# First-image statistics from the framed blocks, and three small reorderings in a convolution-attention and expert kernel

## The chip, the cores and the metric

The kernel runs on one core of one Trainium2 chip. The metric is device time in microseconds (us) of one execution, as a median over runs. Inputs come from HBM and the result goes back to HBM; everything is float32.

## The reference

The input `x` has 4 images of 256 channels and 64 x 64 pixels. Cut to what matters:

```python
# layer 0: group norm, then instance norm, then 3x3 neighbourhood attention
x = x + conv_attn(_gn(x), Wq, bq, Wk, bk, Wv, bv, Wo, bo)
#   xn = (x - mean over h,w) * rsqrt(var over h,w + eps)     per image and channel
#   q = (xn @ Wq + bq) / sqrt(256); k, v = padded xn @ Wk + bk, @ Wv + bv
#   softmax over the 9 neighbours, ctx @ Wo + bo
# layer 1, on 16384 tokens of 256 numbers
t = t + windowed_gated_mean(_ln_t(t), Wp, bp, Wg)             # last 64 tokens
t = t + moe(_ln_t(t), router_w, w1, b1, w2, b2)               # 8 experts, top 2
```

For this change the per-channel mean and variance of a whole image matter: nothing of an image's attention can be computed before all its 4096 pixels per channel have been seen. The kernel folds the two norms of layer 0 and the weights together (`qk` = Wq Wk', `vo` = Wv Wo, `outb` = bo + Wo' bv), and takes the token norm's mean out of the projection by subtracting the weights' own mean over channels (`wpr`).

## The kernel before, in words

An image is cut into 8 blocks of 8 rows (512 pixels), 32 blocks in all. Channels lie on the 128 partitions in two halves (`NC` = 2). A block's pixels come in three layouts, each with its own load on SyncE's queue (SP): `xs` (L151 to L161), 2 x 512 plain pixels per partition, 512 KB, used only for the statistics; `x` (L129 to L139), the block framed by its neighbours, 2 x 10 x 66 per partition, 660 KB, used by the attention; and `xp` (L141 to L146), patches with pixels on partitions, 1 MB.

`channel_stats` (L163) takes `bn_stats` of each channel half of one block on VectorE (DVE); `image_norm` (L420) aggregates the 8 blocks of an image (L423), averages over groups with two small matmuls by `gavg` (L427, L434), takes an inverse square root in some ten tiny DVE steps, and scales `qk` and `ub` by it. Its last part is the "shift products" (L455 to L466): 4 matmuls by `qk` and 8 by `ub`, each over one column (`back` = -mean times the inverse deviation), into the PSUM tile `pqb`; DVE adds them to `qb` and `qbk` (L467 to L470). `edges` (L476) writes the image's mean into the frame of the `x` tile on GpSimd (POOL) and into the patches by DMA.

Then each round of the main loop (L1163) interleaves, step by step, the attention of block g (`attend`), the ranking and dispatch of block g-2 (`ranks`), the windowed layer of block g-1 (`tail`), the queries of block g+1 (`produce`), and a share of the expert slots (`experts`). The expert part scatter-adds its rows to the output with indirect DMAs from POOL (L1094).

What sets the order. Engines run their own instruction streams in order. The tile framework's scheduler makes these streams from the program order and a running priority number; a smaller number goes first among what it believes ready (`tc.cur_priority`). `tc.keep_in_program_order` and `add_manual_dep(... NoSync ...)` only fix an order. DMAs of the SP and ScalarE (ACT) queues share 8 completion semaphores in turn, so the ninth of them isn't issued until the first has landed, and so on: at the start SP's loads and ACT's loads of weights wait for one another in that way.

The start of the kernel is a stage of its own. SP issues the 8 `xs` loads of image 0 (L176 to L178, into the idle buffers of the pools `xs`, `x1`, `wx` and `q`), then 4 `x` loads (L179), a blank block, and two `xp` loads. ACT issues the weights (L190 to L203). TensorE (PE) forms the folded weights (`product`, L387 to L413), which ACT and, for `outb` (L406) and `wpr` (L415), DVE move out of PSUM. DVE has the statistics, the masks (L241 to L261) and these in one stream.

Of the kernel before, what the change touches and what calls it, by code (L numbers as in the profile page):

```python
# [47 lines left out]
AF = mybir.ActivationFunctionType  # L48
# [14 lines left out]
def hybrid_block_kernel(ctx: ExitStack, tc: tile.TileContext, ins: dict, out: bass.AP):  # L63
    nc = tc.nc
    x = ins["x"]
    B, C, FW, _ = x.shape
    W = FW - 2
# [4 lines left out]
    NBI = HW // TB  # L72
# [6 lines left out]
    XBUFS = 4  # L79
    TH, TW = TB // W, 4  # L80
# [31 lines left out]
    xsp = ctx.enter_context(tc.tile_pool(name="xsp", bufs=2))  # L112
    xp = ctx.enter_context(tc.tile_pool(name="xp", bufs=XBUFS))
    xtp = ctx.enter_context(tc.tile_pool(name="xtp", bufs=2))
    xpp = ctx.enter_context(tc.tile_pool(name="xpp", bufs=2))
    w1p = ctx.enter_context(tc.tile_pool(name="w1p", bufs=1))
    w2p = ctx.enter_context(tc.tile_pool(name="w2p", bufs=2))
# [9 lines left out]
    xt, xpat = {}, {}  # L127

    def load_x(g):  # L129

        if g >= NB:
            return
        b, i = divmod(g, NBI)
        t = xp.tile([P, NC, KH, FW], FP, tag="x", name=f"x_{g}")
        nc.sync.dma_start(
            t.rearrange("p c h w -> p c (h w)"),
            x[b, :, i * TH : i * TH + KH, :].rearrange("(c p) h w -> p c (h w)", p=P),
        )
        xt[g] = t  # L139
# [6 lines left out]
        xpat[g] = t  # L146

    xs_of, stats = {}, {}
    idle = (xsp, "xs"), (xtp, "x1"), (w2p, "wx"), (w2p, "q")

    def load_xs(g):  # L151
        if g >= NB:
            return
        b, i = divmod(g, NBI)

        pool, tag = idle[g // 2] if g < NBI else idle[0]
        t = pool.tile([P, NC, TB], FP, tag=tag, name=f"xs_{g}")
        nc.sync.dma_start(
            t, ins["xs"][b, :, i * TB : (i + 1) * TB].rearrange("(c p) n -> p c n", p=P)
        )  # L160
        xs_of[g] = t  # L161

    def channel_stats(g):  # L163

        if g >= NB:
            return
        b, i = divmod(g, NBI)
        t = xs_of.pop(g)
        if i == 0:
            stats[b] = w2p.tile([P, NC, NBI, 6], FP, tag="stats", name=f"stats_{b}")  # L170
        for c in range(NC):
            inst = nc.vector.bn_stats(stats[b][:, c, i, :], t[:, c, :])
            if b:
                tc.keep_in_program_order(inst)

    for g in range(NBI):  # L176
        load_xs(g)
        channel_stats(g)  # L178
    for g in range(XBUFS):  # L179
        load_x(g)  # L180

    def load_const(name, shape, src):
        t = const.tile(shape, FP, tag=name, name=name)
        nc.scalar.dma_start(t, src)
        return t
# [10 lines left out]
    outb = load_const("outb", [P, NC], ins["bo"])  # L196
    A = ins["WpT"].shape[1]

    wpr = const.tile([P, NC, A + E], FP, tag="wpr", name="wpr")
# [65 lines left out]
    for n in range(2):  # L265
        t = const.tile([P, NG, HALF], FP, tag=f"pe_{n}", name=f"pe_{n}")
# [92 lines left out]
    def rsqrt_v(out_, var, eps, n, name):  # L359

        def four(tag, dtype=FP):
            return w4p.tile([P, 4], dtype, tag=tag, name=f"{tag}_{name}")[:, :n]

        ve, guess, t = four("nve"), four("guess", I32), four("nt")
        nc.vector.tensor_scalar_add(ve, var, eps)
        nc.vector.tensor_single_scalar(guess, ve.bitcast(I32), 1, op=ALU.arith_shift_right)
        nc.vector.tensor_scalar(guess, guess, -1.0, float(0x5F3759DF), ALU.mult, ALU.add)
        y = guess.bitcast(FP)
        for last in (False, False, True):
            nc.vector.tensor_mul(t, y, y)  # L370
            nc.vector.scalar_tensor_tensor(t, t, -0.5, ve, ALU.mult, ALU.mult)
            new = out_ if last else y
            nc.vector.scalar_tensor_tensor(new, t, 1.5, y, ALU.add, ALU.mult)
# [13 lines left out]
    def product(dst, pairs, n, name):  # L387
        ps = ps_a.tile([P, n], FP, tag="a", name=f"pw_{name}")
        for k, (lhsT, rhs) in enumerate(pairs):
            nc.tensor.matmul(ps, lhsT, rhs, start=(k == 0), stop=(k == NC - 1))  # L390
        return ps

    for c in range(NC):
        cols = slice(c * P, (c + 1) * P)
        both = range(NC)
        ps = product(qk, [(wqT[:, o, cols], wkT[:, o, :]) for o in both], C, f"qk{c}")
        nc.scalar.mul(qk[:, c, :], ps, SCALE)
        ps = product(qb, [(wkT[:, o, cols], bq[:, o : o + 1]) for o in both], 1, f"qb{c}")
        nc.scalar.mul(qb[:, c : c + 1], ps, SCALE)
        ps = product(vo, [(wvT[:, o, cols], wo[:, o, :]) for o in both], C, f"vo{c}")  # L400
        nc.scalar.copy(vo[:, c, :], ps)
        ps = product(ucol, [(wqT[:, o, cols], bk[:, o : o + 1]) for o in both], 1, f"u{c}")
        nc.scalar.mul(ucol[:, c : c + 1], ps, SCALE)
        nc.gpsimd.tensor_copy(ub[:, c, :], ucol[:, c : c + 1].to_broadcast([P, 32]))
        ps = product(outb, [(wo[:, o, cols], bv[:, o : o + 1]) for o in both], 1, f"outb{c}")
        nc.vector.tensor_add(outb[:, c : c + 1], outb[:, c : c + 1], ps)  # L406
    ps = product(qbk, [(bqb[:, o, :], bk[:, o : o + 1]) for o in range(NC)], 1, "qbk")
    nc.scalar.mul(qbk, ps, SCALE)

# [2 lines left out]
    nc.gpsimd.memset(mean_c, 1.0 / C)  # L412
    ps = product(wpr, [(mean_c, wpr[:, ci, :]) for ci in range(NC)], A + E, "wpr")  # L413
    for ci in range(NC):
        nc.vector.tensor_sub(wpr[:, ci, :], wpr[:, ci, :], ps)  # L415


    norm, mean_row, ask = {}, {}, {}
# [1 line left out]
    def image_norm(b):  # L420
        mv = w2p.tile([P, NC, 2], FP, tag="imv", name=f"imv_{b}")
        for c in range(NC):
            nc.vector.bn_aggr(mv[:, c, :], stats[b][:, c].rearrange("p i s -> p (i s)"))  # L423
        mean = w2p.tile([P, NC], FP, tag="imean", name=f"imean_{b}")
        nc.vector.tensor_copy(mean, mv[:, :, 0])
        gm = ps_a.tile([P, NC], FP, tag="a", name=f"gm_{b}")
        nc.tensor.matmul(gm, gavg, mean, start=True, stop=True)  # L427

        spread = w2p.tile([P, NC], FP, tag="ispread", name=f"ispread_{b}")
        nc.vector.tensor_sub(spread, mean, gm)  # L430
        nc.vector.tensor_mul(spread, spread, spread)
        nc.vector.tensor_add(spread, spread, mv[:, :, 1])
        gv = ps_a.tile([P, NC], FP, tag="a", name=f"gv_{b}")
        nc.tensor.matmul(gv, gavg, spread, start=True, stop=True)  # L434


        vc = w2p.tile([P, NC], FP, tag="ivc", name=f"ivc_{b}")
        nc.vector.scalar_tensor_tensor(vc, gv, EPS, mv[:, :, 1], ALU.mult, ALU.add)
        rc = w2p.tile([P, NC], FP, tag="irc", name=f"irc_{b}")
        rsqrt_v(rc, vc, EPS * EPS, NC, f"c{b}")  # L440
        back = w2p.tile([P, NC], FP, tag="iback", name=f"iback_{b}")
        nc.vector.scalar_tensor_tensor(back, mean, -1.0, rc, ALU.mult, ALU.mult)
        norm[b] = (mean, rc, back)
        row = mean_row[b] = hbm.tile([1, C], FP, tag=f"mean_row_{b}", name=f"mean_row_{b}")
        nc.sync.dma_start(row.rearrange("o (c p) -> p (o c)", p=P), mean)


        qks = w2p.tile([P, NC, C], FP, tag="qks", name=f"qks_{b}")
        ubs = w2p.tile([P, NC, 32], FP, tag="ubs", name=f"ubs_{b}")
        for c in range(NC):  # L450
            nc.scalar.mul(qks[:, c, :], qk[:, c, :], rc[:, c : c + 1])
            nc.gpsimd.tensor_scalar_mul(ubs[:, c, :], ub[:, c, :], rc[:, c : c + 1])
        qbb = w2p.tile([P, NC], FP, tag="qbb", name=f"qbb_{b}")
        ps = ps_a.tile([P, NC + 1], FP, tag="a", name=f"pqb_{b}")
        for co in range(NC):  # L455
            for ci in range(NC):
                nc.tensor.matmul(
                    ps[:, co : co + 1], qk[:, ci, co * P : (co + 1) * P], back[:, ci : ci + 1],
                    start=(ci == 0), stop=(ci == NC - 1),
                )  # L460
        for n in range(NG):
            for ci in range(NC):
                nc.tensor.matmul(
                    ps[32 * n : 32 * (n + 1), NC:], ub[:, ci, :], back[:, ci : ci + 1],
                    start=(ci == 0), stop=(ci == NC - 1),
                )  # L466
        nc.vector.tensor_add(qbb, qb, ps[:, 0:NC])  # L467
        nc.vector.tensor_mul(qbb, qbb, rc)
        kb = w2p.tile([P, 1], FP, tag="kb", name=f"kb_{b}")
        nc.vector.tensor_add(kb, qbk, ps[:, NC:])  # L470
        ask[b] = qks, qbb, ubs, kb
# [663 lines left out]
    for g in range(2):  # L1135
        load_xp(g)
    image_norm(0)
    edges(0)
    edges(1)
# [21 lines left out]
    for g in range(*stats_at[0]):  # L1161
        load_xs(g)
# [79 lines left out]
```

## Time and profile before

| | us |
|---|---|
| median of 19 runs (lowest to highest) | 1299.82 (1295.74 to 1303.95) |
| the profiled execution, its own time | 1305.36 |
| its span, first to last instruction | 1303.7 |
| PE busy, share of the span | 1140.2, 87% |
| DVE busy | 926.8, 71% |
| ACT busy | 824.4, 63% |
| POOL busy | 703.4, 54% |
| mean granted TensorE clock | 0.953 |

The profiled execution is 5.5 us above the median and 1.4 us above the highest of the runs. A line of the timeline has the start, the duration, the engine, the source line, the operation, output <- inputs with shapes, and in square brackets the idle time of that engine just before, with what ended it. SPq is SyncE's queue of DMA issues; PEld is the weight load of a matmul. A float32 matmul has two records.

### The profile page before, as it was taken

What the parts mean: (1) busy time and instruction counts of PE and PEld (TensorE: products, weight loads), DVE (VectorE), ACT (ScalarE), POOL (GpSimd) and SP (SyncE); (2) the same over time, 40 slices, a digit from 0 to 9 for tenths busy, and PEclk for the clock granted to TensorE, in tenths of its full rate; (3) what the DMA queues carried; (4) which work ended last, traced back from release to release, by engine and by line L of the source; (5) the groups of instructions that cost most, each with busy time, mean ns of one, the idle gap of its engine ahead of it and who ended that gap; (6) DMA issues with size and microseconds to landing.
All of it is one profiled execution on the core that took longest, in us unless ns stands there. A gap on an engine that the chain in (4) does not pass through costs nothing. (4 is left out here: it accounts for less than half of the span.)

```text
span 1303.7 us, 28100 instructions
## 1 busy us (share of the span) xinstructions
PE 1140.2 (87%) x8620; PEld 813.9 (62%) x8620; DVE 926.8 (71%) x4650; ACT 824.4 (63%) x1633; POOL 703.4 (54%) x615
## 2 busy tenths in 40 slices
PE   4977879999999999999999999999999999767660
PEld 4544556666767767676766676667676666656550
DVE  4488878978888888788878688878876798422220
ACT  1454557768777867787877678787867775423320
POOL 2013233666665657565656566666675667654443
PEclk9988879999999999999999899999999999878995
DMA  9774556777776777767777576667756556755543
GB/s 325 225 249 152 169 163 163 189 192 179 171 191 134 185 209 174 179 177 185 172 156 177 131 181 163 168 171 164 179 111 141 116 125 124 178 110 84 83 63 36
DMA packets 138723, 209.99 MB, mean 161 GB/s; under 512 B 15712, under 2 KB 108752, under 8 KB 134352
## 3 DMA queue, kind: packets, MB, share of 16 engines
q1 hardware_dynamic: 84912, 135.81, 34.2%
q0 software_dynamic: 51168, 71.07, 30.0%
q8 instruction: 71, 1.16, 0.4%
q10 hardware_dynamic: 2496, 1.32, 0.4%
q14 instruction: 76, 0.62, 0.2%
HBM read 117.56 MB, written 90.59 MB: 160 GB/s over the span
## 5 line engine op out<-in xcount | busy, mean ns | idle before, releaser
L1094 POOL DMA_INDIRECT out<-sx x270 | 427.9, 1585 | 380.2 <-DVE sx L1081 108.6
L892 POOL DMA_INDIRECT rows_in<-tok,rows x256 | 254.9, 996 | 139.8 <-issue 74.4
L1076 PE MATMUL psy<-w,h 128*128 x1080 | 292.5, 394 | 30.5 <-DVE sx L1080 29.1
L1076 PEld LDWEIGHTS psy<-w,h 128*128 128x128 f32 x1080 | 196.6, 193 | 126.5 <-DVE sx L1080 60.5
L1057 PE MATMUL psh<-xc,w1s 128*128 128x256 f32 x1080 | 271.5, 394 | 2.8 <-ACT h L1063 2.5
L1080 DVE TENSOR_TENSOR sx<-psy,b2b 128x256 f32<-128x256 f32 x270 | 113.8, 421 | 182.9 <-PE psy L1076 177.0
L1057 PEld LDWEIGHTS psh<-xc,w1s 128*128 128x128 f32 x1080 | 202.4, 195 | 50.3 <-issue 9.3
L1063 ACT ACTIVATE h<-psh,w1s 128x256 f32<-128x256 f32 x270 | 113.0, 469 | 94.0 <-PE psh L1057 93.1
L1045 PE MATMUL ptx<-ident,sx 128*128 128x128 f32 x540 | 86.5, 282 | 46.3 <-DMA sx<-rows_in 46.3
L660 PE MATMUL pso<-mixT,vo 128*128 128x512 f32 x256 | 126.2, 609 | 0.0
L518 PE MATMUL psq<-x,qks 128*128 128x512 f32 x256 | 125.8, 612 | 0.0
L1049 ACT COPY xc<-ptx 128x512 f32<-128x512 f32 x135 | 78.6, 582 | 69.9 <-PE ptx L1045 69.6
L1045 PEld LDWEIGHTS ptx<-ident,sx 128*128 128x128 f32 x540 | 67.9, 148 | 66.6 <-issue 47.1
L1081 DVE TENSOR_SCALAR sx<-sx 128x256 f32<-128x256 f32 x270 | 100.3, 371 | 4.3
L1038 ACT COPY w1s<-w1b 128x514 f32 x135 | 83.6, 629 | 2.7 <-ACT xc L1049 0.4
L791 ACT ACTIVATE x<-x,scale 128x256 f32<-128x256 f32 x128 | 66.4, 590 | 26.9 <-DVE scale L787 23.4
L523 ACT ACTIVATE q<-psq,qbb,irc 128x512 f32<-128x512 f32 x64 | 49.6, 775 | 47.6 <-PE psq L518 47.4
L1063 ACT ACT_TABLE_LOAD x60 | 77.0, 1283 | 0.9
L697 PE MATMUL psp<-wpr,x1c 128*128 128x136 f32 x512 | 73.0, 285 | 4.5 <-DVE so_far L868 2.9
L697 PEld LDWEIGHTS psp<-wpr,x1c 128*128 128x128 f32 x512 | 66.9, 192 | 10.1 <-ACT q L523 5.6
L751 PE MATMUL psw<-wx,band 128*64 128x512 f32 x128 | 72.4, 666 | 0.0
L748 PE MATMUL psw<-wl,bandl 128*64 128x512 f32 x128 | 72.4, 666 | 0.0
(224 smaller groups left out, 1983.8 us busy)
## 6 DMA issues: line engine op xcount, KB each, us to landing
sx<-rows_in SPq DMA_DIRECT2D x135, 272.0 KB
xp<-in_xp SPq DMA_DIRECT2D x32, 1024.0 KB
x<-in_x SPq DMA_DIRECT2D x32, 660.0 KB
xs<-in_xs SPq DMA_DIRECT2D x32, 512.0 KB
out<-x SPq DMA_DIRECT2D x32, 512.0 KB
out<-sx POOLq DMA_INDIRECT x270, 4.2
rows_in<-tok,rows POOLq DMA_INDIRECT x256, 2.6
rows_in<-blank SPq DMA_DIRECT2D x9, 272.0 KB
```

The source lines that it names most:

```text
L518: nc.tensor.matmul(ps.rearrange("p (r w) -> p r w", w=W), qks[:, ci, co * P : (co + 1) * P], t[:, ci, 1 : TH + 1, 1 : W + 1], start=(ci == ...
L660: nc.tensor.matmul(ps, vo[:, ci, co * P : (co + 1) * P], mixT[:, ci, :], start=(ci == 0), stop=(ci == NC - 1),)
L697: nc.tensor.matmul(ps[:, u, :], xc[:, ci, t * P : (t + 1) * P], wpr[:, ci, :], start=(ci == 0), stop=(ci == NC - 1),)
L892: return nc.gpsimd.indirect_dma_start(out=rows_in[:, :], out_offset=bass.IndirectOffsetOnAxis(ap=rows[:, c, t : t + 1], axis=0), in_=tok[: ...
L1038: nc.scalar.copy(w1s, w1b[:, e, :])
L1045: nc.tensor.transpose(pt[:, c, t * P : (t + 1) * P], xs[:, t, c * P : (c + 1) * P], ident)
L1057: nc.tensor.matmul(ps[:, f, :], w1s[:, o : o + P], xc[:, ci, :], start=(ci == 0), stop=(ci == NC - 1),)
L1063: inst = nc.scalar.activation(h[:, f, :], ps[:, f, :], AF.Gelu, bias=w1s[:, F1 + f : F1 + f + 1])
L1076: nc.tensor.matmul(ps[:, t, :], h[:, f, t * P : (t + 1) * P], w2[:, e, f, :], start=(f == 0), stop=(f == NC - 1),)
L1080: nc.vector.tensor_add(ys[:, t, :], ps[:, t, :], b2b[:, e, :])
L1081: nc.vector.tensor_scalar_mul(ys[:, t, :], ys[:, t, :], xs[:, t, bass.ds(e + C, 1)])
L1094: inst = nc.gpsimd.indirect_dma_start(out=out, out_offset=bass.IndirectOffsetOnAxis(ap=xs[:, t, C + E : C + E + 1].bitcast(U32), axis=0), ...
```

## The change

Blocks 0 to 3 of image 0 are no longer loaded as `xs`; their statistics read the inside of the framed `x` tiles, which are loaded first. Blocks 4 to 7 are still loaded as `xs`, now into the pools `xs` and `x1` alone. The addition of Wo' bv to `outb` goes from DVE to ACT. The subtraction of the weights' mean is put behind the last statistics of image 0 in DVE's stream. The 12 shift products get a priority number that is 60 larger, for every image.

```diff
-    idle = (xsp, "xs"), (xtp, "x1"), (w2p, "wx"), (w2p, "q")
+    idle = (xsp, "xs"), (xtp, "x1")
...
-        pool, tag = idle[g // 2] if g < NBI else idle[0]
+        pool, tag = idle[(g - XBUFS) // 2] if g < NBI else idle[0]
...
-        t = xs_of.pop(g)
+        t = xs_of.pop(g, None)
+        if t is None:
+            t = xt[g][:, :, 1 : TH + 1, 1 : W + 1]
...
+        return inst
 
     for g in range(NBI):
-        load_xs(g)
-        channel_stats(g)
-    for g in range(XBUFS):
-        load_x(g)
+        (load_x if g < XBUFS else load_xs)(g)
+        counted = channel_stats(g)
...
-        nc.vector.tensor_add(outb[:, c : c + 1], outb[:, c : c + 1], ps)
+        nc.scalar.activation(
+            outb[:, c : c + 1], ps, AF.Identity, bias=outb[:, c : c + 1]
+        )
...
-        nc.vector.tensor_sub(wpr[:, ci, :], wpr[:, ci, :], ps)
+        inst = nc.vector.tensor_sub(wpr[:, ci, :], wpr[:, ci, :], ps)
+        tc.add_manual_dep(
+            inst.ins, counted.ins.name,
+            mybir.DependencyInfo(
+                mybir.DependencyClass.NoSync, mybir.DependencyReason.SCHED_ONLY
+            ),
+            reason="behind the first image's statistics",
+        )
...
+        at = tc.cur_priority
+        tc.cur_priority = at + 60
         for co in range(NC):
...
                     start=(ci == 0), stop=(ci == NC - 1),
                 )
+        tc.cur_priority = at
         nc.vector.tensor_add(qbb, qb, ps[:, 0:NC])
```

## The prediction

> **What bounds the kernel now.** I read the page's busy shares and slices first, then the stages by windows, the timeline of DVE and PE up to 36 us, and the four places of the shift products. PE is the bound in the middle (194.6 of the 200 us from 600 to 800), so what PE starts earlier ends earlier; the last 100 us are a chain of POOL's scatter-adds, which shifts with the rest.
>
> The start is bound otherwise. DVE's timeline from 15.5 us:
>
> ```profile
> 15.62 0.15 DVE L406 TENSOR_TENSOR outb<-outb,pw_outb 128x1 f32<-128x1 f32 x1 [4.29 <-PE pw_outb L390]
> ...
> 22.00 0.16 DVE L406 TENSOR_TENSOR outb<-outb,pw_outb 128x1 f32<-128x1 f32 x1 [2.83 <-PE pw_outb L390]
> 22.08 1.28 DVE L172 BATCH_NORM_STATS2 stats<-xs 128x6 f32<-128x512 f32 x2
> 23.27 0.18 DVE L257 TENSOR_SCALAR near<-near 128x60 f32<-128x60 f32 x1
> 23.97 0.30 DVE L415 TENSOR_TENSOR wpr<-wpr,pw_wpr 128x136 f32<-128x136 f32 x1 [0.52 <-PE pw_wpr L390]
> ...
> 25.81 1.28 DVE L172 BATCH_NORM_STATS2 stats<-xs 128x6 f32<-128x512 f32 x2
> 27.01 0.58 DVE L423 BATCH_NORM_AGGREGATE imv<-stats 128x2 f32<-128x48 f32 x2
> ```
>
> Statistics stand behind small additions that wait for PE: 4.29 + 2.83 + 0.52 = 7.6 us of idle DVE. The loads are not late: the trace's DMA packets show the last xs row in at 20.9 us, and its statistics start 4.9 us later. PE follows on the mean:
>
> ```profile
> 22.68 1.25 PE L390 MATMUL pw_wpr<-wpr,mean_c 128*128 128x136 f32 x4
> 27.94 0.56 PE L427 MATMUL gm<-imean,gavg 128*128 128x2 f32 x2 [4.00 <-DVE imean L425]
> ...
> 34.82 2.07 PE L518 MATMUL psq<-x,qks 128*128 128x512 f32 x2
> ```
>
> From 27.01 to 34.82 nothing but a chain of tiny steps runs, the same in both kernels. The transfers by windows (the last two columns are the DMA share and GB/s):
>
> ```profile
> 14.00:16.00 2.00, 1.75 (x10) 1.67 (x8) 0.34 (x4) 0.62 (x4) 0.36 (x2) 1.00 0.37 76
> ...
> 20.00:28.00 8.00, 4.00 (x19) 3.62 (x17) 5.26 (x17) 0.71 (x3) 0.35 (x2) 1.00 1.05 397
> ```
>
> **Part 1, the start.** Removed: four xs loads (2,048 KB). In their place the four x loads, 660 KB each and needed anyway, go first. So 4 x 660 + 4 x 512 = 4,688 KB lie ahead of the last statistics and not 4,096: 592 KB or 0.61 MB more, at 397 GB/s 1.5 us. The last xs lands at 20.9 + 1.5 = 22.4. From the first xs row's landing (4.73) to its statistics (5.76) 1.03 us passed, and a pair of statistics takes 1.28: done at 24.7. I take the strided rows of 64 at the same price; at double, only the last pairs matter, and those are plain xs.
>
> The two subtractions of wpr now stand ahead of the aggregation; they take 0.5 us together and need pw_wpr, which PE ends at 23.9. Without DVE's outb addition in the way PE could be 0.25 us earlier; with x packets of 2,640 B beside the weights (xs: 2,048), the weights land later. Bounds: 23.7, and 25.2 if the weights' loads, spread from 2.6 to 10.3 us, stretch by a sixth. I take 24.7, the middle of a late half, since bq lies behind all four weights on its queue. Aggregation then begins at 24.7 + 0.5 = 25.2 and not 27.01: **-1.8 us**. The two outb additions on ACT (0.17 us each, from the row of qb on ACT) lie in ACT's wait for PE. Bounds for the part: -2.7 (the 76 GB/s hole at 14 to 16 us fills, PE at 23.7) and +0.4 (the eight shared DMA semaphores make x_3 wait for Wo and the later xs for bv, bo and WpT; the last xs then lands 2.2 us after my 22.4).
>
> Does the gain stay? The x tiles are there. The patches' frames need the stored mean, which SP issued at 27.82 behind 2 MB of xp; it waited 10.2 us for it, and the first patches were still whole before psc needed them at 47.24. All of that moves earlier. w1b, the experts and later blocks are issued behind steps that shift. SP's mean store passes no new load; POOL's frame copy (0.30 us) moves past three others and is needed 6 us later.
>
> **Part 2, the shift products of images 1 to 3.** The order listing shows that the first of the 12 keeps its place behind iback, so PE's waits there (0.4, 0.3 and 0.7 us before the weight load) stay. The other 11 go some 25 instructions later; DVE's qbb and kb go with them, so DVE no longer waits for PE. At image 3:
>
> ```profile
> 725.28 1.22 PE L457 MATMUL pqb<-iback,qk 128*128 128x1 f32 x8 [0.33 <-DVE iback L442]
> 726.43 0.42 PE L463 MATMUL pqb<-iback,ub 128*32 128x1 f32 x16
> ```
>
> and on DVE
>
> ```profile
> 726.97 0.16 DVE L467 TENSOR_TENSOR qbb<-qb,pqb 128x2 f32<-128x2 f32 x1 [1.40 <-PE pqb L463]
> ```
>
> DVE's waits are 0.81, 1.46 and 1.40. PE ran on without a gap behind the first two; behind the third an expert's sx L1081 was held up, so I count that one: **-1.4**; bounds 0 and -3.7.
>
> The cost: in image 1 the products land among psp, which uses the whole array too: 0. In images 2 and 3, however, the listing has them one by one between the last eight psc products. Those run side by side:
>
> ```profile
> 196.10 1.89 PE L518 MATMUL psq<-x,qks 128*128 128x512 f32 x4
> 197.92 1.09 PE L632 MATMUL psc<-xp,pT 60*32 60x256 f32 x32
> 198.94 0.38 PE L697 MATMUL psp<-wpr,x1c 128*128 128x136 f32 x1
> ```
>
> Four psq records of 512 columns take 1.82 us, so a psc of 256 columns and two records would alone take 0.455; yet 16 took 1.02 us, or 0.064 each. No row shows them split. Bounds: 0, and 8 x (0.455 - 0.064) = 3.1 an image. I count what stays side by side in the listing, six stretches: 6 x 0.455 = 2.7, and 0.5 for products not hidden, against 1.02 + 1.24 now: +1.0 an image, **+2.0**. The Trainium skill's page TensorEngine Tiling, section Key Properties, says that a change of tiling mode drains TensorE; that speaks against this edit, gives no price, and points to the upper bound, by which the sum would end slower. psq to psc, one such change above, shows about 0.1 us.
>
> The clock, by windows around image 3 (busy times of PE, PEld, DVE, ACT, POOL, then the granted clock):
>
> ```profile
> 723.00:726.00 3.00, 1.93 (x12) 1.39 (x11) 2.43 (x15) 2.75 (x7) 2.52 (x2) 1.00 0.64 70
> 726.00:730.00 4.00, 4.00 (x32) 3.45 (x32) 2.10 (x12) 1.77 (x4) 2.92 (x4) 0.50 0.40 122
> ```
>
> Behind 3 us with much of PE in waits and one-column products the clock halves, from 726.0 to 732.9: 3.4 us of work lost. Images 1 and 2 show no such drop of their own. Spread out, the products may no longer tip it. I count half, **-1.7**; bounds 0 and -3.4. The page TensorE: Matmul & The Clock Gate, section The HAM clock gate, asks for an idle window of about 3.4 us for a drop; no PE gap here is over 0.8 us, and the measurement decides. By the page this term is 0 and the sum -1.2.
>
> **The sum.** -1.8 - 1.4 + 2.0 - 1.7 = -2.9 us: 1305.4 becomes 1302.5 for the profiled execution. That execution is 5.5 us above the median, in no stage that the change touches, so the median goes from 1299.8 to **1296.9**.
>
> **Rivals.** (a) The start gains, the rest cancels or is absorbed: PE's idle time between 60 and 150 us (20 us, waiting for ACT's wl copies) can swallow a shift, and DVE's waits cost nothing. Then -1.8 + 2.0 or 0, or about 1299. For it: PE never paused behind two of the three waits. Against: those stages are chains that begin with image 0's first block. (b) Slower: split psc products lose all that ran side by side, in images 2 and 3. 6.3 - 1.8 - 1.4 = +3.1, or 1302.9. It decides against the change from 3.2 + 2.6 = 5.8 us of loss on, if the clock stays as it is. For it: a full-array product stands between neighbours; against: those with ub use 32 columns and need not stop the others. (c) The order does not do what it says: x_3 waits for Wo, the mean comes at 27, part 1 is 0; about 1299.0.
>
> **How the numbers follow.** A measurement of this kernel tells about 0.2%, 2.6 us, from no change. Forecast 0.45 (faster), (a) 0.22 and (c) 0.10 (same), (b) 0.23 (slower by over 0.2% in nearly all of it): faster 0.45, same 0.33, slower 0.22. Low: both better bounds, 2.7 + 1.4 + 1.7 + 1.1 (half the splitting cost saved) = 6.9: 1292.9. High: rival (b), 1302.9. Forecast's own range 1294 to 1299.
>
> **What would show it.** Right: the aggregation near 25.2 us and psq near 33; DVE's idle time ahead of qbb near zero; full clock behind image 3's products; psc in images 2 and 3 some 2 us longer. Wrong: wpr waiting past 26.5 us for PE, statistics waiting for xs past 24, or psc stretches of 4 us.

## The result, and the profile after

The changed kernel takes **1316.2 us** (median of 7 runs, 1315.1 to 1322.2) against 1299.6 for the kernel before beside it: a ratio of **1.0137, 95% interval 1.0120 to 1.0154**. The forecast was 1296.9 in a range up to 1302.9. The profiled execution took 1315.94 us by its own time, its span is 1314.2, and the mean granted clock 0.948 (before 0.953).

**The start came out as forecast, a little better.** The timeline of VectorE (DVE), of the changed kernel:

```profile
19.88 3.93 DVE L174 BATCH_NORM_STATS2 stats<-xs 128x6 f32<-128x512 f32 x6
23.73 0.48 DVE L418 TENSOR_TENSOR wpr<-wpr,pw_wpr 128x136 f32<-128x136 f32 x2
24.13 0.60 DVE L433 BATCH_NORM_AGGREGATE imv<-stats 128x2 f32<-128x48 f32 x2
```

No wait for TensorE (PE) is left there: the last three pairs of statistics run back to back, and the aggregation begins at 24.13 where it was 27.01, 2.9 us earlier (forecast: 1.8). PE had wpr's product ready before DVE came to it, and psq moved by the same amount:

```profile
21.50 1.25 PE L391 MATMUL pw_wpr<-wpr,mean_c 128*128 128x136 f32 x4
...
31.96 2.93 PE L531 MATMUL psq<-x,qks 128*128 128x512 f32 x3
```

The hole in the transfers that before had from 14 to 16 us (76 GB/s) is filled, as the better bound of the start supposed. A line of the windows has the stretch, its length, the busy time of PE, PEld, DVE, ACT and POOL with the number of instructions, the granted clock, the DMA share and GB/s:

```profile
14.00:16.00 2.00, 2.00 (x7) 1.82 (x8) 0.24 (x3) 0.42 (x2) 0.36 (x2) 1.00 0.90 249
```

**Nearly all of the loss lies in three places.** I set the start of each PE instruction of the changed kernel against the same instruction of before. PE is 2.9 us ahead at the first psq and 4.5 us ahead at 188 us. At image 1 it loses 1.5 us. From there to 450 us the lead moves by 1.1 us only. At image 2 (450 to 465 us) 1.9 us ahead becomes 5.5 us behind, a loss of 7.4; at image 3 (725 to 745 us) 6.8 behind becomes 12.4, a loss of 5.6. The span ends 10.5 us later. Elsewhere the difference drifts by up to 4 us, to either side. The execution profiled of before lay 5.8 us above its median, that of after on its median, so 10.5 + 5.8 = 16.3 of the 16.6 us between the medians are accounted for.

At image 2 before had the whole block of psc in one line, and the products in one run ahead of it (1.24 us):

```profile
456.63 1.09 PE L632 MATMUL psc<-xp,pT 60*32 60x256 f32 x32
457.65 1.19 PE L697 MATMUL psp<-wpr,x1c 128*128 128x136 f32 x8
```

PE's timeline of the changed kernel there:

```profile
453.84 0.66 PE L645 MATMUL psc<-xp,pT 60*32 60x256 f32 x16
454.43 0.38 PE L469 MATMUL pqb<-iback,qk 128*128 128x1 f32 x2
454.74 0.62 PE L645 MATMUL psc<-xp,pT 60*32 60x256 f32 x2
455.29 0.38 PE L469 MATMUL pqb<-iback,qk 128*128 128x1 f32 x2
455.60 0.62 PE L645 MATMUL psc<-xp,pT 60*32 60x256 f32 x2
...
457.00 0.22 PE L475 MATMUL pqb<-iback,ub 128*32 128x1 f32 x2
457.16 0.62 PE L645 MATMUL psc<-xp,pT 60*32 60x256 f32 x4
457.71 0.22 PE L475 MATMUL pqb<-iback,ub 128*32 128x1 f32 x2
457.86 0.62 PE L645 MATMUL psc<-xp,pT 60*32 60x256 f32 x2
458.41 0.22 PE L475 MATMUL pqb<-iback,ub 128*32 128x1 f32 x2
...
459.55 0.26 PE L475 MATMUL pqb<-iback,ub 128*32 128x1 f32 x2
459.74 1.06 PE L645 MATMUL psc<-xp,pT 60*32 60x256 f32 x2
460.73 0.38 PE L475 MATMUL pqb<-iback,ub 128*32 128x1 f32 x8
461.04 2.18 PE L710 MATMUL psp<-wpr,x1c 128*128 128x136 f32 x8
```

Read the differences of the first column. Eight psc together (16 records) take 0.59 us. After that the other eight stand in seven stretches: six of one psc and, at 457.16, one of two. From 454.74 to 455.29 it is **0.55 us for one psc**, nearly what eight took, and the two together take 0.55 as well. A product by `qk` takes 0.31 us (455.29 to 455.60), one by `ub` 0.16. A pair is 0.86 or 0.70 us at full clock. The last pair shown, 459.55 to 460.73, takes 1.18 us: the clock is halved. The stretch from 453.84 to 461.04 is 7.2 us; before, the psc took 1.02 us and the eleven products that now stand between them 1.0. None of these lines has a bracket, so PE waited for nothing; it was busy throughout.

At image 3 it is much the same (nine psc together, then seven alone), and the windows show where the forecast half of a clock drop went:

```profile
736.00:740.00 4.00, 4.00 (x19) 1.82 (x18) 1.15 (x7) 0.84 (x2) 3.32 (x5) 0.80 0.27 75
740.00:744.00 4.00, 4.00 (x21) 1.51 (x21) 0.19 (x3) 0.52 (x2) 1.62 (x1) 0.50 1.06 275
744.00:748.00 4.00, 4.00 (x11) 2.67 (x11) 1.32 (x9) 0.32 (x1) 0.00 (x0) 0.50 0.54 127
```

The clock is halved for 10.2 us from 738 (before: 6.8 us from 726), and for 6.8 us from 459, where before had none. DVE's wait at qbb did not go: it grew from 1.46 us (image 2) and 1.40 us (image 3) to

```profile
461.17 0.16 DVE L480 TENSOR_TENSOR qbb<-qb,pqb 128x2 f32<-128x2 f32 x1 [4.42 <-PE pqb L475]
```

and 6.45 us. In DVE's stream qbb did move: in before it stands behind iback, in the changed kernel behind the token norm's statistics and most of its small steps. The last product moved further still. At image 1, where the products lie among psp, DVE does not wait for them.

### The profile page after: what moved, and what is told of

The parts are those of the page before. It is cut to its first block, busy times and chain, and to the rows that moved or that the text cites. A ratio compares the mean times of both kernels' runs of the same rounds, so it can differ in the third digit from the quotient of the medians.

```text
span 1314.2 us, 28095 instructions
## 1 busy us (share of the span) xinstructions
PE 1156.3 (88%) x8620; PEld 820.1 (62%) x8620; DVE 927.5 (71%) x4648; ACT 826.3 (63%) x1635; POOL 704.9 (54%) x615
```

## The experiments

Theory S: the loss is the splitting of psc that had run side by side. Rivals: the lateness itself, by DVE's wait at qbb (W); the clock alone (R2); and that the early start is paid for later (L). The first four kernels ran on one chip (before there 1296.9), the next four on a second (1296.4), the last four on a third, which runs the kernel before in 1339.5; only ratios are compared across them.

**e1: the change without the priority number.**

```diff
-        at = tc.cur_priority
-        tc.cur_priority = at + 60
...
-        tc.cur_priority = at
```

> The change without the larger priority number: framed statistics, outb on ScalarE and the wpr subtraction stay, the 12 shift products stand together at their old place. Theory S (the loss is made where one-column products split psc products that ran side by side, in images 2 and 3): all of the loss is gone and the start's 2.9 us of gain stays, so 1296 to 1298 us, with a lead of 2 to 4 us over before that is kept behind images 1, 2 and 3. Rival L (something in the start, such as the later loads, costs time further on): still slower than before, above 1305 us.

Measured: 1294.0 us, ratio 0.9983 (0.9967 to 0.9998). The whole loss is gone and the start's gain is there, so L falls.

**e2: before with the priority number alone.**

```diff
+        at = tc.cur_priority
+        tc.cur_priority = at + 60
...
+        tc.cur_priority = at
```

> The kernel before with the larger priority number alone. Theory S: the loss without the start's gain, 1316 + 3 = 1319 us, with steps of some 7 us at image 2 (near 455 us) and at image 3 (near 730 us). Rival L: near 1300 us.

Measured: 1313.8 us, ratio 1.0138 (1.0113 to 1.0162), as much as the whole change. PE loses 5.9 us at image 2 and 5.7 at image 3 in its trace, with psc split in the same way. At image 2 the block of psc and products stands there at nearly full clock (0.98):

```profile
453.32:459.60 6.28, 6.28 (x55) 2.87 (x55) 3.08 (x16) 1.82 (x4) 4.18 (x5) 0.98 0.66 172
```

It takes 6.28 us against some 2.0 for the same instructions in before, so over 4 us of loss are there without the clock, and R2 alone can't be the cause. The priority number is the cause; S and W are left.

**e3: the number 80 in place of 60.**

```diff
-        tc.cur_priority = at + 60
+        tc.cur_priority = at + 80
```

> The changed kernel with 80 in place of 60: the 11 products come still later in TensorE's order, behind all psc products, which stay whole in all images; qbb waits on VectorE as in the changed kernel. Theory S: 1296 to 1299 us, no step at images 2 and 3. Rival W (the loss comes from the lateness itself: VectorE's wait at qbb and the PSUM tile that is held longer): at least as slow as the changed kernel, 1316 us or more.

Measured: 1299.8 us, ratio 1.0016 (0.9999 to 1.0033). The products are later than in the change, and the psc are whole. Its PE timeline at image 2:

```profile
455.56 1.09 PE L645 MATMUL psc<-xp,pT 60*32 60x256 f32 x32
456.58 0.83 PE L469 MATMUL pqb<-iback,qk 128*128 128x1 f32 x6
457.34 0.30 PE L475 MATMUL pqb<-iback,ub 128*32 128x1 f32 x8
457.57 0.50 PE L710 MATMUL psp<-wpr,x1c 128*128 128x136 f32 x2
458.00 0.22 PE L475 MATMUL pqb<-iback,ub 128*32 128x1 f32 x2
458.15 0.50 PE L710 MATMUL psp<-wpr,x1c 128*128 128x136 f32 x2
```

Most of the loss is gone with the splits, though the products come later still, so the lateness itself is not what costs. But DVE hardly waits at qbb here (0.09 us at most at images 1 to 3; the expectation had it waiting), so this run does not tell the splits from DVE's wait. And e3 is still 5.8 us behind e1, for S alone too much. The lines show a part of it: psp is split now, and that costs too. A psp product (2 records) and a `ub` product take 0.58 us in place of 0.26 (8 records in 1.03) and 0.03 (a run of 16 records in 0.26). Four such pairs are 1.2 us an image. The clock is halved for 3.4 us behind images 1 and 2, 1.7 us each. So matmuls that use the whole array and do not run side by side pay for being split as well, some 0.3 us a pair.

**e4: the number 40.**

```diff
-        tc.cur_priority = at + 60
+        tc.cur_priority = at + 40
```

> The changed kernel with 40 in place of 60: now the products split the psc products of image 1 (12 of 16 stand alone) and leave those of images 2 and 3 whole. Theory S: one step, at image 1 (near 195 us), of 5 to 8 us, and none at images 2 and 3: 1302 to 1305 us. Rival W: the products are less late in all images, so some loss in each, and none larger at image 1.

Measured: 1310.3 us, ratio 1.0088 (1.0061 to 1.0114). Now it is image 1 that is split, into eleven stretches of one or two psc and a last one of four; images 2 and 3 are whole. PE's timeline at image 1, the first and the last of them:

```profile
191.40 0.62 PE L645 MATMUL psc<-xp,pT 60*32 60x256 f32 x2
191.95 0.38 PE L469 MATMUL pqb<-iback,qk 128*128 128x1 f32 x2
...
201.76 1.06 PE L645 MATMUL psc<-xp,pT 60*32 60x256 f32 x2
202.75 0.27 PE L475 MATMUL pqb<-iback,ub 128*32 128x1 f32 x2
202.94 1.08 PE L645 MATMUL psc<-xp,pT 60*32 60x256 f32 x8
203.95 2.18 PE L710 MATMUL psp<-wpr,x1c 128*128 128x136 f32 x8
```

The 16 psc and the products between them take 12.55 us, and PE loses 12.8 us at image 1, 0.7 at image 2 and nothing at image 3. The loss goes where the splits go. The clock is halved for 13.7 us from 195, which makes the loss larger than the splits alone.

**e5: DVE's additions of the shift products put into attend, behind psc in the program.**

```diff
-        tc.cur_priority = at + 60
+        tc.cur_priority = at + 57
...
-        nc.vector.tensor_add(qbb, qb, ps[:, 0:NC])
...
+        def shifts():
+            nc.vector.tensor_add(qbb, qb, ps[:, 0:NC])
...
+        if late:
+            late.pop()()
```

> The changed kernel with VectorE's two additions of the shift products put into the next block's attention instead of ahead of it, so that TensorE's stream is that of the changed kernel, instruction for instruction, with the same eight products between the psc, while VectorE no longer stands at qbb for 4.4 us. Theory S (the psc that ran side by side are split; a pair of one psc and one product takes 0.70 to 0.86 us at full clock and 1.18 at half): the loss stays whole, ratio to before 1.011 to 1.016 (1311 to 1318 us if before is 1297 to 1300), and the psc stretches of images 2 and 3 stay at 7 us. Rival W (the late products hurt because VectorE waits for them and what stands behind it is late): 3 to 4.4 us an image come back, ratio 1.003 to 1.007.

Measured: 1314.6 us, ratio 1.0125 (1.0103 to 1.0146). With the number at 57, PE's stream has the same splits as the change. But the wait did not go, since the scheduler kept qbb where the change has it in DVE's stream: 4.07 us at image 2 and 6.58 at image 3. So this run does not tell S from W, and a kernel with the splits but without the wait was not tried. The traces at hand do tell: a wait of DVE can cost time only where PE, the bound here, stands idle for it. These are the 50 us from 10 us ahead of qbb at images 2 and 3, first of before, then of the change:

```profile
443.83:493.83 50.00, 47.27 (x390) 34.01 (x392) 39.34 (x212) 34.06 (x72) 30.17 (x27) 1.00 0.69 181
716.97:766.97 50.00, 48.29 (x361) 33.55 (x362) 38.63 (x207) 33.17 (x71) 29.99 (x26) 0.93 0.60 139
451.17:501.17 50.00, 47.97 (x349) 31.70 (x351) 31.46 (x162) 27.74 (x57) 26.76 (x24) 0.90 0.67 179
733.81:783.81 50.00, 49.67 (x395) 32.31 (x398) 32.50 (x168) 28.03 (x58) 26.38 (x23) 0.90 0.58 148
```

PE is idle for 2.03 and 0.33 us in the change, less than the 2.73 and 1.71 of before. So DVE's wait is not where the loss comes from.

**e6 and e7: the start in its two halves.** e6 has the framed statistics and loads alone, e7 the two small moves (outb on ScalarE, wpr behind the statistics) alone; neither has the priority number.

```diff
+        (load_x if g < XBUFS else load_xs)(g)
+        counted = channel_stats(g)
```

```diff
+        nc.scalar.activation(
+            outb[:, c : c + 1], ps, AF.Identity, bias=outb[:, c : c + 1]
+        )
...
+        tc.add_manual_dep(
+            inst.ins, counted.ins.name,
```

> Before with the framed statistics and loads alone: outb stays on VectorE, wpr's subtractions stay where the scheduler puts them, no priority number is changed. By VectorE's stream four pairs of statistics (4 x 1.23 us) now stand behind the first subtraction of wpr, which waits for pw_wpr (22.75 in the changed kernel): 22.75 + 0.3 + 4.9 + 0.5 = 28.4, later than 27.01. Theory order (the start's 2.9 us come from taking the waits for TensorE out of VectorE's statistics): aggregation at 27.5 to 29, time +0.5 to +2 us of before, ratio 1.000 to 1.0015. Rival loads (the gain comes from the 1,456 KB that no longer lie ahead in the queue): aggregation at 24 to 25.5, ratio 0.997 to 0.999.

> Before with the two small moves alone: outb's additions on ScalarE and wpr's subtractions behind the last statistics; eight xs loads as before, no priority number is changed. The last xs landed at 20.9 in before. Theory order: statistics end at 22.5 to 23, pw_wpr at 23.5, aggregation at 23.7 to 24.5, thus 2.5 to 3.3 us ahead of before; ratio 0.997 to 0.999 (2 to 4 us). Rival loads: aggregation stays past 26, ratio 1.000.

Measured: e6 1297.9 us, ratio 1.0013 (0.9999 to 1.0026); e7 1296.3 us, ratio 0.9988 (0.9973 to 1.0004). DVE's timelines, e6 first:

```profile
21.50 0.16 DVE L407 TENSOR_TENSOR outb<-outb,pw_outb 128x1 f32<-128x1 f32 x1 [2.54 <-PE pw_outb L391]
23.47 0.30 DVE L416 TENSOR_TENSOR wpr<-wpr,pw_wpr 128x136 f32<-128x136 f32 x1 [1.81 <-PE pw_wpr L391]
...
28.96 0.35 DVE L424 BATCH_NORM_AGGREGATE imv<-stats 128x2 f32<-128x48 f32 x1
```

```profile
21.48 1.29 DVE L172 BATCH_NORM_STATS2 stats<-xs 128x6 f32<-128x512 f32 x2
23.39 0.50 DVE L418 TENSOR_TENSOR wpr<-wpr,pw_wpr 128x136 f32<-128x136 f32 x2 [0.62 <-PE pw_wpr L391]
23.81 0.60 DVE L433 BATCH_NORM_AGGREGATE imv<-stats 128x2 f32<-128x48 f32 x2
```

With the loads alone, the statistics still stand behind additions that wait for PE (2.54 + 1.81 us), and the aggregation is 2 us later than before. With the moves alone it is at 23.81, 3.2 us earlier than before, and no later than in the whole change. The start's gain is the order of DVE's stream. Neither time can be told from before by itself; e7 against e6 is 0.0025 or 3.2 us of the 5.1 us between their aggregations.

**e8: the number 20.**

```diff
-        tc.cur_priority = at + 60
+        tc.cur_priority = at + 20
```

> The changed kernel with 20 in place of 60: the eleven products of images 1 to 3 go behind the ptp and the first ptx transposes, in one run and ahead of psc, so none is between psc. Theory S: no split psc, no loss, ratio 0.997 to 0.999, as the changed kernel without any priority (0.9983); psc of images 2 and 3 take 1.0 to 1.1 us. Rival R2 (late one-column products bring the clock down wherever they stand): a half-clock stretch of 3.4 to 6.8 us behind images 2 and 3, 1.7 to 3.4 us each, ratio 1.000 to 1.004. If VectorE's wait at qbb (0.8 to 1.5 us in before) were on the path, this kernel would be some 0.5 to 1 us ahead of or behind the one without priority.

Measured: 1296.8 us, ratio 0.9999 (0.9983 to 1.0014). PE's timeline at image 2:

```profile
451.23 0.73 PE L469 MATMUL pqb<-iback,qk 128*128 128x1 f32 x6
451.89 0.33 PE L475 MATMUL pqb<-iback,ub 128*32 128x1 f32 x16
...
454.06 1.09 PE L645 MATMUL psc<-xp,pT 60*32 60x256 f32 x32
```

Eleven products in one run, late, and psc whole: no loss. Each `qk` product of the run costs 0.22 us, each `ub` product 0.03. DVE waits 2.50 us at qbb there, 1 us more than before, and PE changes by 0.4 us against before across that image. So neither a late run of one-column products nor a longer wait on DVE costs anything that shows; with the windows under e5, W falls. Nor does the clock drop at any of the three images, so products that are late, but in one run, do not bring it down. The small gain that S expected is not there either; the start's gain alone is too near the bound of what this measures.

**e9, e10, e11 and e12: how the loss grows with the number of gaps.** Three kernels without the priority number put the 12 products of images 1 to 3 into one gap behind the eighth psc, into four gaps of three, or into eight gaps of one (the rest behind the last psc). The order is pinned, and an expert's psh and psy come into the first gap in all three. e12 is e1 again, as their measure. The core of the edit, for four gaps:

```diff
+                    if late:
+                        behind(inst)
+                        first.append(inst)
+                    if late and (pair, half, j) in ((0, 1, 3), (1, 0, 1), (1, 0, 3), (1, 1, 1)):
+                        late[0][0](3)
```

> The changed kernel without the priority numbers, and in images 1 to 3 all 12 shift products put, in one run, between the eighth and the ninth psc of the image's first block; the order is pinned, and an expert's psh and psy come to stand in the same gap. First of three kernels that differ only in how many gaps the 12 products are spread over (1, 4, 8). Theory S, priced from the changed kernel (a psc alone 0.55 us, a stretch of eight 0.6): the last eight psc still take 0.6 us, the run of products 1.3; against the kernel without priority at most 0.5 us an image, ratio to before 0.998 to 1.002. Rival T (any foreign product in the block ends the side by side run for what follows): the last eight psc take 4 us here too, ratio 1.007 or more.

> The same, with the 12 products in four gaps of three: behind psc 8, 10, 12 and 14, so that the last eight psc stand in four stretches of two. Theory S: two psc on different columns still run side by side, a stretch costs about what one alone costs (0.55 to 0.6 us), so 4 x 0.6 = 2.4 us for the last eight, and 0.1 us per gap for products no longer in a run: 2.2 us an image more than with one gap, 6 to 7 us for three images, some more where the clock drops; ratio 0.004 to 0.008 above that of one gap. Rival T: as with one gap.

> The same, with eight gaps: each of the last eight psc stands alone between two products, as in images 2 and 3 of the changed kernel, but in image 1 too. Theory S: at full clock 4 x 0.86 + 4 x 0.70 us for the pairs against 0.6 + 1.3 with one gap, so 4.3 us an image more, 13 us in all, and up to 3.4 us an image more where the clock is halved in it: 13 to 23 us above one gap, ratio 0.010 to 0.018 above it. Rival W2 (the loss lies in what stands behind the products, not in their number): eight gaps within 3 us of one gap.

> The changed kernel without the priority numbers once more, as the measure for the three with gaps, and to see whether it stays ahead of before: ratio 0.9983 was measured (0.9967 to 0.9998). Theory start (2.9 to 3.8 us earlier at the aggregation, most of it kept): 0.997 to 0.999. Rival (the start's gain is swallowed by TensorE's waits between 60 and 150 us): 0.9995 to 1.001.

| | us | ratio to before (1339.5) | products and last eight psc, image 1 |
|---|---|---|---|
| e12, products ahead of psc | 1338.9 | 0.9989 (0.9971 to 1.0007) | |
| e9, one gap | 1333.0 | 0.9953 (0.9931 to 0.9976) | 1.80 us |
| e10, four gaps | 1342.7 | 1.0021 (1.0001 to 1.0040) | 3.91 us |
| e11, eight gaps | 1356.6 | 1.0124 (1.0094 to 1.0153) | 8.23 us |

PE's timelines at image 1, e9 and then e10:

```profile
186.39 1.02 PE L482 MATMUL pqb<-iback,qk 128*128 128x1 f32 x8 [0.35 <-DVE nve_a L366]
187.35 0.33 PE L482 MATMUL pqb<-iback,ub 128*32 128x1 f32 x16
187.60 0.66 PE L662 MATMUL psc<-xp,pT 60*32 60x256 f32 x16
188.19 1.19 PE L735 MATMUL psp<-wpr,x1c 128*128 128x136 f32 x8
```

```profile
189.10 0.80 PE L482 MATMUL pqb<-iback,qk 128*128 128x1 f32 x6 [0.34 <-DVE nve_a L366]
189.83 0.62 PE L662 MATMUL psc<-xp,pT 60*32 60x256 f32 x4
190.38 0.38 PE L482 MATMUL pqb<-iback,qk 128*128 128x1 f32 x2
190.70 0.29 PE L482 MATMUL pqb<-iback,ub 128*32 128x1 f32 x4
```

A stretch of eight psc takes 0.59 us (187.60 to 188.19), a stretch of two 0.55 (189.83 to 190.38), one alone 0.55. The price is **0.55 us a stretch, however many psc are in it up to eight**, and the loss goes by the number of gaps. Three more gaps cost 2.1 us at image 1 (2.2 expected) and 9.7 us of the median, more than three times 2.1; behind image 2 e10 has 6.8 us of half clock where e9 has 3.4. Seven more gaps cost 6.4 us at image 1, two of them for the half clock that begins at 191 us and lasts 10.2, and 23.6 us of the median, just above the 13 to 23 that were expected. The rival T (one foreign product ends the gain for the whole block) falls with e9.

e9 was not meant as a better kernel, yet it is the fastest against before, 0.5% below it. Its trace has an expert's psh and psy between the psc and the products that wait for `iback`; whether this is why was not tested.

## Why the prediction was wrong

**Part 1, "Aggregation then begins at 25.2": right, and a little small.** It began at 24.13. The statistics were done at 23.7 and not at 24.7, and wpr's product, which I had also put at 24.7, was through at 22.75. Strided statistics cost 1.29 us, as I took them. Rival (c), x_3 held up by the semaphores, did not come. e7 shows that the two small moves make this gain, and that the framed loads, for which I had reckoned 1.5 us of transfers, add nothing that these runs can tell. In the time it is small: e1 0.9983, e12 0.9989, e8 0.9999, against the 0.9986 that 1.8 us would be.

**Part 2, "+1.0 an image, +2.0": this step failed.** It counted "what stays side by side in the listing, six stretches" at 0.455 us, and 0.5 for the products: 3.2 us for a block. The trace has eight stretches in each image, the first of eight or nine psc. Each of the other seven costs 0.55 us, and each product between them 0.31 or 0.16 us and not the 0.22 or 0.03 of a run. At full clock that is 0.59 + 3 x 0.86 + 4 x 0.70 + 0.12 for the last four products = 6.1 us for image 2; e2 measured 6.28. Before, the same instructions took 1.02 + 1.0, so it is **+4.1 us and not +1.0**. (The 1.24 us that the forecast set against its 3.2 hold the first product too, 0.24 us, which stays at its place.) At image 3 the first nine take 0.98 in place of 0.59: +4.5. The sign of being wrong, "psc stretches of 4 us", is there: 7.2 and 8.7 us. My upper bound of 3.1 us an image had left out the products and took a lone psc at 0.455. The argument that products by `ub` "need not stop the others" is refuted by the lines from 457.71: a psc between two of them takes 0.55 us (457.86 to 458.41) like any other.

**"In image 1 the products land among psp [...]: 0" was too low.** It cost 1.5 us. e3 shows the price, some 0.3 us for each psp with a `ub` product behind it.

**"DVE's waits, -1.4": wrong in sign.** I held that qbb goes later with the products. It did, but not as far as the last of them, and the wait grew to 4.42 and 6.45 us. It costs little in itself, as e8 shows for 2.50 us and the windows under e5 for both; behind it at image 2 stand the token norm's last step and pj, and pj then waits another 1.73 us for psp.

**The clock, "I count half, -1.7": wrong in sign.** Where the products were spread out, the clock fell: 6.8 us of half clock at image 2, 10.2 at image 3, or 3.4 + 5.1 us of lost work against the 3.4 of before. Every kernel in which psc stand one by one has 10 to 14 us of half clock at one image at least (the change, e2 and e5 10.2 at image 3, e4 13.7 at image 1, e11 10.2 at all three). With psc whole it is 0 (e8) to 3.4 us at an image, apart from the 6.8 of before at image 3; of that drop e1 has half, and e6, e7 and e8 have none. I had taken what one execution did for a property of the kernel. What in the splits lowers the clock is open: PE counts as busy all the while (4.00 of 4.00), so idle time of PE is not what these profiles show ahead of the drop.

Together: splits 4.1 + 4.5, clock 3.4 + 1.7 net of before, image 1 1.5, make 15.2 us; the traces show 7.4 + 5.6 + 1.5 = 14.5. So two terms of the sum failed by about as much: the splits were put at +2.0 and cost 8.6, the clock at -1.7 and cost 5.1. Rival (b) named the splits and their direction, with a chance of 0.23; it reckoned 6.3 us for them and left the clock as it is.

The Trainium skill says, in TensorEngine Tiling, section Key Properties, that a change of tiling mode drains TensorE. The runs fit this, with a number: in e3 a psp and a `ub` product in alternation take 0.29 us more than in runs. The larger part is the lost overlap: a lone psc takes 0.55 us, and eight on different tiles 0.59.

## What to carry to other kernels

Small matmuls that run side by side on tiles are to be priced by the stretch, not by the piece: what is put between them costs a whole stretch each time, here 0.55 us plus its own 0.16 to 0.31, and a few such microseconds brought the clock down besides. So before a priority number is moved, read from the listing which run it lands in, count the gaps it makes, and price a gap by a lone instruction, with what stands in it; keep fillers in one run ahead of or behind the block. And a term that rests on one event of one profiled execution, like the clock drop here, is not to be counted on until a second execution shows it.

## What was not expected of the hardware

- One psc of 256 columns takes 0.55 us, two on different tiles 0.55, eight 0.59, sixteen 1.02 us.
- The granted clock halves for up to 13.7 us while PE is busy without a gap, where isolated tiled matmuls alternate with one-column products (e4, from 195 us); a run of the same products does not do it (e8).
- A third chip ran the kernel before 3% slower (1339.5 against 1296.4 us), and ratios kept their order: the change without the priority number is at 0.9983 on the first chip and 0.9989 there.
